# Toeplitz blocks of 64 rows: a channel pair in the row halves of the array, its tables on two DMA queues

## The chip, the core and the metric

The kernel runs on one core of one Trainium2 chip. The metric is device time in microseconds (us) of one launch: the median of three runs before the change is 2316.38 us (2315.62 to 2317.1). A profile is one execution recorded by the hardware profiler; it names PE (TensorE matmul), PEld (TensorE weight load), DVE (VectorE), ACT (ScalarE), POOL (GpSimd) and SP (SyncE, which here only issues DMAs and reads registers).

## What is computed

`x` is 32 sequences of 64 channels of 1024 samples. Four residual layers follow one another; the change lies in the first alone.

```python
def _L0_cond_ref(u, log_dt, C, log_A_real, A_imag, D, length):
    K = _get_kernel(log_dt, C, log_A_real, A_imag, Lq)     # one filter of 1024 taps a channel
    y = jnp.fft.irfft(rfft(u, n=2*Lq) * rfft(K, n=2*Lq)[None], n=2*Lq)[..., :Lq]
    y = y + u * D[:, None]
    mask = (jnp.arange(Lq)[None, :] < length[:, None])
    return y * mask[:, None, :]
...
x = x + _L0_cond_ref(x, ...)                      # causal convolution, masked
x = x + einsum('bsi,boi->bso', x, weight1[ids1])  # an adapter matrix 1024x1024 for each sequence
x = x + einsum('bij,bkj->bik', x, weight2[ids2])  # another
x = x + gated_mlp_with_low_rank_adapters(x)       # the rest of the time
```

## The kernel before

**Stages.** The work falls into the convolution of all 64 channels for all 32 sequences; the two adapter layers of the first chunk of 8 sequences (`adapters(0)`, L297 to L345); and the gated MLP of the four chunks, into which the adapters of later chunks are woven. The profile shows them at 20 to 194 us, 194 to 330 us, and 330 us to the end.

**Making the filters.** `kernels(g)` (L1315) makes the filters of one group of channels; `GROUPS` are 4, 4, 8, 8, 8, 8, 8, 8, 8, here called sets 0 to 8. A set is a loop through several engines: POOL raises powers, DVE reduces an angle (`br`, L1177 to L1181), ACT takes absolute value, sine and cosine with table loads between (`bk` L1186, `bsi` L1328, `bco` L1187 and L1330, `brho` L1249), DVE multiplies (`bet`, `bgt` L1341), PE contracts (`pk`, L1346 and L1355), ACT copies out of PSUM (`ks`, L1364) and issues the store to DRAM (`kp`, L1366). Set g+2 is made while set g is convolved (`more`, L1445).

**Convolving.** A causal convolution is a product with a Toeplitz matrix. `convolve` (L1372) treats 4 channels (`HA`). For each channel it reads from DRAM a table `hk` with one shifted copy of the filter in each partition: partition p starts one sample after partition p-1, so that any 128 columns of it are a 128x128 Toeplitz block. With the reversed samples `uf` as moving operand, 8 matmuls (L1404) of 256, 224, ... 32 columns sum over the block diagonals d = 0 to 7 of one channel. In the profile each such fp32 matmul is two records, so a channel is 16 records on PE, and a pair of channels 32. There are 32 pairs, here numbered 0 to 31. DVE multiplies a pair's PSUM bank by the mask (`tmp`, L1172), POOL adds it to `x` (L1419) for the first chunk, copies the other chunks' share (L1422) and stores it (L1423).

**Order.** PE follows the source order (`manual_schedule(engines={PE})`, L129). The other engines' orders come from a planner. Each engine works through its own list in order, DMA issues among it: an issue that waits holds back everything behind it on that engine. SP issues all of `uf` (a buffer of two), `hk` (a buffer of three pairs) and the adapter weights; ACT issues only the stores `kp`. Eight completion semaphores are taken in turn by the DMAs of SP and ACT together, and a DMA waits for the one eight before it.

**Weights ahead.** Adapter weights are 128 tiles of 512 KB for the first chunk. 9 rotating buffers (`ROTATING`) and a number of resident ones (`early`: `EARLY` of their own and 4 in the place of a later `x` tile; `LATE` more once the filters are made) are filled during the convolution: 36 tiles in all, by `fetch` (L207), whose calls are spread over the convolution by `FIRST_LOADS` and `MORE_LOADS` (L1394 to L1398); what is left is issued after the last table. The other 92 tiles come while `adapters(0)` runs, each when PE has used up a rotating buffer.

Of the kernel before, what the change touches and what calls it, by code (L numbers as in the profile page):

```python
# [9 lines left out]
F32 = mybir.dt.float32  # L10
# [4 lines left out]
SP = mybir.EngineType.SP  # L15
# [4 lines left out]
P = 128  # L20
B, H, L = 32, 64, 1024
NS = 64
KT = L // P
# [8 lines left out]
MB = 4  # L32
MG = 2
NG = FM // MG
EARLY = 16
LEFT_AT = 11
LATE = 7
FIRST_LOADS = 8
MORE_LOADS = 3
ROTATING = 9  # L40
HA = 4
SEG = 2
# [10 lines left out]
KROW = P + L  # L53
# [23 lines left out]
def kernel(  # L77
# [55 lines left out]
    epool = first.enter_context(tc.tile_pool(name="epool", bufs=1, side="right"))  # L133
    early = [epool.tile([P, L], F32, tag=f"e{i}", name=f"early{i}") for i in range(EARLY)]
    early += [
# [75 lines left out]
    def places():  # L211

        lpool = first.enter_context(tc.tile_pool(name="lpool", bufs=1, side="right"))
        for i in range(LATE):
            early.append(lpool.tile([P, L], F32, tag=f"l{i}", name=f"late{i}"))

    convolution(tc, cst, consts, xt, xf, ssm, lens, xs[0], cd, ps_tile, fetch, places)
    for _ in before:
        pass
# [911 lines left out]
def convolution(tc, cst, consts, xt, xf, ssm, lens, x0, cd, ps_tile, fetch, places):  # L1131
# [9 lines left out]

    nc = tc.nc
    with ExitStack() as ctx:
        g0 = ctx.enter_context(tc.tile_pool(name="g0", bufs=1))
        g0_2 = ctx.enter_context(tc.tile_pool(name="g0_2", bufs=2))
        making = ExitStack()
# [2 lines left out]
        s3 = ctx.enter_context(tc.tile_pool(name="s3", bufs=3))  # L1149
# [14 lines left out]
        def small():  # L1164
            n_small[0] += 1
            return s1.tile([P, H], F32, tag=f"sm{n_small[0]}", name=f"sm{n_small[0]}")
# [4 lines left out]
        def tt(o, a, b, op):  # L1171
            nc.vector.tensor_tensor(o, a, b, op)  # L1172
            return o
# [80 lines left out]
        x, y = small(), small()  # L1254
# [6 lines left out]
        t, em, ep = small(), small(), small()  # L1261
# [110 lines left out]
        def convolve(kp, row, ha, between):  # L1372


            uf = s3.tile([P, HA, KT, B], F32, tag="uf", name=f"uf{ha}", bufs=2)
            nc.sync.dma_start(uf, xf[:, ha : ha + HA])
            if ha == 0:
                fetch(FIRST_LOADS)
            tmp = g0_2.tile([P, HA, KT * B], F32, tag="tmp", name=f"tmp{ha}")
            for i in range(0, HA, 2):  # L1380
                hk = s3.tile([P, 2, L], F32, tag="hk", name=f"hk{ha + i}")

                for j in range(0, 2, 1 if ha == 0 else 2):
                    n = 1 if ha == 0 else 2
                    nc.sync.dma_start(
                        hk[:, j : j + n],
                        bass.AP(
                            tensor=kps.tensor,
                            offset=kp[row + i + j : row + i + j + 1, 1:2].offset,
                            ap=[[1, P], [KROW, n], [1, L]],  # L1390
                        ),
                    )

                first, last = ha <= HA * MORE_LOADS, ha > H - HA * MORE_LOADS  # L1394
                if ha and i == 0:
                    fetch(1 + first)
                elif ha and last:
                    fetch(1)  # L1398
                if i:
                    between()  # L1400
                ps = ps_tile(f"pc{ha + i}").rearrange("p (i t) -> p i t", i=2)
                for j in range(2):
                    for d in range(KT):
                        nc.tensor.matmul(  # L1404
                            ps[:, j, d * B :],
                            hk[:, j, d * P : (d + 1) * P],
                            uf[:, i + j, : KT - d, :].rearrange("p k b -> p (k b)"),
                            start=(d == 0),
                            stop=(d == KT - 1),
                        )  # L1410
                tt(
                    tmp[:, i : i + 2, :],
                    ps,
                    maskf.unsqueeze(1).to_broadcast([P, 2, KT * B]),
                    ALU.mult,
                )
            xv = x0.rearrange("p k (b h) -> p k b h", h=H)[:, :, :, ha : ha + HA]
            tv = tmp.rearrange("p i (k b) -> p k b i", b=B)[:, :, :BC, :]
            nc.gpsimd.tensor_tensor(xv, xv, tv, ALU.add)  # L1419
            co = g0.tile([P, NCK - 1, HA * KT, BC], F32, tag="co", name=f"co{ha}")  # L1420
            tv = tmp.rearrange("p i (k c b) -> p c (i k) b", k=KT, b=BC)[:, 1:]
            nc.gpsimd.tensor_copy(co, tv)  # L1422
            nc.gpsimd.dma_start(  # L1423
                cd.rearrange("c p g e -> p c g e")[:, :, ha // HA],
                co.rearrange("p c i b -> p c (i b)"),
            )
# [14 lines left out]
        maskf = mask.rearrange("p k b -> p (k b)")  # L1441
        for g, n in enumerate(GROUPS):
            h0 = sum(GROUPS[:g])

            def more():  # L1445
                if len(ready) < min(g + 3, len(GROUPS)):
                    ready.append(kernels(len(ready)))
                    if len(ready) == len(GROUPS):
                        making.close()
                        places()  # L1450

            for i in range(0, n, HA):
                convolve(ready[g], i, h0 + i, more)
# [20 lines left out]
def _layouts(np, v):  # L1474
    cont = np.ascontiguousarray

    x = v["x"]

    xt = x.reshape(NCK, TC, KT, P).transpose(3, 0, 2, 1)

    xf = x.reshape(B, H, KT, P)[..., ::-1].transpose(3, 1, 2, 0)

    def states(a):
        return np.concatenate([a.T, a.T])
# [58 lines left out]
    for i, (m0, m1) in enumerate(BLOCKS):  # L1543
        n = 2 * (m1 - m0)
        ad[:, i, :, :n] = a[:, :, :, m0:m1].reshape(NE, P, n, R)
    left = left.reshape(P + REST, NE, R).transpose(1, 0, 2)
    n = 2 * BLOCKS[0][1]
# [71 lines left out]
```

## Time and profile before

The profiled execution has a span of 2313.8 us, 2.6 us under the median of the runs.

| what | from | value |
|---|---|---|
| PE, PEld busy over the span | the page's part 1 | 2249.8 us (97%), 1868.0 us (81%) |
| DVE, ACT, POOL busy | part 1 | 1320.6, 380.0, 270.6 us |
| mean granted TensorE clock | cores | 0.998 |
| all DMA | part 3 | 684.96 MB, 296 GB/s |
| `hk` tables | part 6, DMA view | 30 of 1024 KB, 8.8 us to landing; 4 of 512 KB, 6.6 us |
| `kp` stores on ACT's queue | DMA view | 7 of 32 KB, 7.9 us to landing; 2 of 16 KB, 3.2 us |
| `uf`, `early` loads | DMA view | 512 KB each, 5.8 and 9.4 us to landing |
| DVE mask product `tmp` | groups | 32 of 688 ns |
| first and last convolution matmul | tile view of `pc` | start at 29.1 and 193.8 us |

In the rows of groups the columns are line, engine, operation, output and inputs by name, shape, count; then busy time in us and the mean of one in ns; then idle time of the engine just before, with what ended it. In a timeline a row is start, duration, engine, line, operation, operands, count, and in brackets the idle time before it with its cause.

### The profile page before, as it was taken

To read this page: it belongs to the slowest core of one execution; us is meant where nothing else is said; L and a number is where in the kernel's file an instruction comes from. 1 tells how busy PE (TensorE), PEld (TensorE's weight loads), DVE (VectorE), ACT (ScalarE), POOL (GpSimd) and SP (SyncE) were. 2 spreads that over 40 slices of the span, in tenths; PEclk is the share of its full clock that TensorE was granted. 3 is DMA by queue.
4 is the path that set the end of the run, shared out by engine and by line. 5 is a ranking of instruction groups with operands and counts; after the bars stand their busy time and mean duration, and the time that the engine had idled before them with its cause. 6 is when DMAs were issued, how large, how long until landed. Compare 5 with 4: busy or idle time off the path is not lost.

```text
span 2313.8 us, 53743 instructions
## 1 busy us (share of the span) xinstructions
PE 2249.8 (97%) x21706; PEld 1868.0 (81%) x21706; DVE 1320.6 (57%) x2791; ACT 380.0 (16%) x822; POOL 270.6 (12%) x388
## 2 busy tenths in 40 slices
PE   5999989999999999999999999999999999999999
PEld 4996557787777789688778889688769889799998
DVE  7511127567446776546535676646535676477585
ACT  4300001011001112111102212121102212121220
POOL 3423003111101121000000011000000011100000
PEclk9999999999999999999999999999999999999999
DMA  8999997879997957879997957879997947285582
GB/s 306 354 370 394 407 403 280 317 289 354 365 343 293 350 174 258 304 285 360 350 357 279 358 167 265 297 292 358 355 351 288 363 152 276 87 298 203 191 280 68
DMA packets 201802, 684.96 MB, mean 296 GB/s; under 512 B 26178, under 2 KB 28482, under 8 KB 201042
## 3 DMA queue, kind: packets, MB, share of 16 engines
q1 hardware_dynamic: 169714, 590.77, 69.5%
q0 software_dynamic: 25184, 82.37, 9.6%
q10 hardware_dynamic: 6656, 8.39, 1.0%
q8 instruction: 171, 2.80, 0.5%
q14 instruction: 77, 0.63, 0.1%
HBM read 614.02 MB, written 67.40 MB: 295 GB/s over the span
## 4 chain that ended last, share of the span: by engine, by line
PE 78%; DMA 14%; issue 5%; DVE 2%; POOL 1%; POOLq 0%; SPq 0%; ACT 0%; DVEq 0%
PE pq L664 28%; PE po L1063 22%; PE pa L304 11%; DMA wa<-in_w 7%; PE pc L1404 5%; PE pf L573 5%; PE pr L797 3%; DMA wa<-sums 2%; DMA sums<-kept 1%; PE pe L456 1%; DMA hk<-kp 1%; PE pl_d L427 1%; DMA kp<-ks 1%; DMA wf<-in_wg 0%; DMA wr<-in_wr 0%
## 5 line engine op out<-in xcount | busy, mean ns | idle before, releaser
L304 PE MATMUL pa<-wa,x 128*32 128x256 f32 x7760 | 449.1, 381 | 19.3 <-DMA wa<-in_w 16.8
L664 PE MATMUL pq<-xd,wa 128*128 128x128 f32 x3360 | 415.9, 275 | 1.3 <-DMA wa<-sums 0.9
L304 PEld LDWEIGHTS pa<-wa,x 128*32 128x32 f32 x7760 | 241.8, 110 | 209.9 <-DMA wa<-in_w 49.1
L664 PEld LDWEIGHTS pq<-xd,wa 128*128 128x128 f32 x3360 | 395.0, 192 | 2.3 <-DMA wa<-sums 2.2
L664 PE MATMUL pq<-xd,wb 128*128 128x128 f32 x2520 | 324.1, 276 | 0.6 <-DVE x L316 0.4
L664 PEld LDWEIGHTS pq<-xd,wb 128*128 128x128 f32 x2520 | 300.7, 192 | 4.7 <-DVE x L316 0.6
L314 DVE STREAM_TRANSPOSE y<-pa 128x512 f32<-128x512 f32 x64 | 45.9, 717 | 286.6 <-PE pa L304 286.6
L1063 PE MATMUL po<-act,wd 128*128 128x256 f32 x640 | 168.6, 386 | 0.0
L1404 PE MATMUL pc<-uf,hk 128*128 128x256 f32 (+7 forms) x1024 | 153.3, 312 | 12.2 <-DMA hk<-kp 9.5
L1063 PE MATMUL po<-actd,s 128*128 128x256 f32 x640 | 164.2, 379 | 0.0
L1063 PE MATMUL po<-actd,wd 128*128 128x256 f32 x640 | 164.2, 379 | 0.0
L1404 PEld LDWEIGHTS pc<-uf,hk 128*128 128x128 f32 x1024 | 148.4, 195 | 16.6 <-issue 7.9
L355 POOL DMA_INDIRECT bgu<-in_bgu,rows x44 | 51.4, 1168 | 924.0 <-PE pe L456 827.2
L573 PE MATMUL pf<-xd,wf 128*128 128x256 f32 x640 | 150.9, 381 | 0.0
L1063 PEld LDWEIGHTS po<-act,wd 128*128 128x128 f32 x640 | 117.8, 190 | 29.9 <-issue 14.6
L482 DVE TENSOR_TENSOR s<-wd 128x256 f32<-128x256 f32 x80 | 33.8, 423 | 184.1 <-PE po L1063 184.0
L573 PEld LDWEIGHTS pf<-xd,wf 128*128 128x128 f32 x640 | 121.2, 191 | 17.4
L1063 PEld LDWEIGHTS po<-actd,s 128*128 128x128 f32 x640 | 121.6, 190 | 16.5
L1063 PEld LDWEIGHTS po<-actd,wd 128*128 128x128 f32 x640 | 121.6, 190 | 16.5
L1095 ACT COPY uo<-po 128x256 f32<-128x256 f32 x48 | 17.9, 373 | 622.3 <-PE po L1063 620.2
L573 PE MATMUL pf<-xd,s 128*128 128x256 f32 x480 | 115.9, 385 | 3.9 <-DVE up L607 2.7
L573 PEld LDWEIGHTS pf<-xd,s 128*128 128x128 f32 x480 | 91.0, 191 | 20.0 <-DVE up L607 4.4
(235 smaller groups left out, 2566.4 us busy)
## 6 DMA issues: line engine op xcount, KB each, us to landing
wa<-in_w SPq DMA_DIRECT2D x485, 512.0 KB, 7.0
wa<-sums SPq DMA_DIRECT2D x210, 512.0 KB, 5.8
wb<-parts SPq DMA_DIRECT2D x120, 384.0 KB, 5.3
wd<-in_wd SPq DMA_DIRECT2D x80, 512.0 KB, 7.0
wb<-in_wq SPq DMA_DIRECT2D x90, 384.0 KB, 5.9
hk<-kp SPq DMA_DIRECT2D x30, 1024.0 KB, 8.8
sums<-kept POOLq DMA_DIRECT2D x30, 1024.0 KB, 7.2
wf<-in_wg SPq DMA_DIRECT2D x20, 512.0 KB, 7.1
```

Of the source, the lines that this page charges most:

```text
L304: nc.tensor.matmul(acc[i * S : (i + 1) * S, s * 256 : (s + 1) * 256], xs[c][:, kt, lo + s * S : lo + (s + 1) * S], wt[:, i * 256 : (i + 1) ...
L314: nc.vector.transpose(y, acc)
L355: nc.gpsimd.indirect_dma_start(out=t, out_offset=None, in_=table, in_offset=bass.IndirectOffsetOnAxis(ap=at_, axis=0),)
L427: nc.tensor.matmul(ps[pair(j)], at[:, i, pair(j)], x_i[:, 2 * H * j : 2 * H * (j + 1)], start=(i == 0), stop=(i == n - 1),)
L456: nc.tensor.matmul(ps[:, at_ * 2 * H : (at_ + 1) * 2 * H], bt[pair(j), g], tms[table][pair(j)], start=(g == 0), stop=True, skip_group_chec ...
L482: nc.vector.tensor_add(s1, a21, a22)
L573: nc.tensor.matmul(ps, ws[j][:, kt, :], xb[j][:, kt, :], start=start and kt == 0, stop=kt == KH - 1, skip_group_check=True,)
L664: nc.tensor.matmul(ps[:, to * TQ : (to + 1) * TQ], w[i][:, k, :], xb[:, j, SLOT[i], k, :], start=start and k == 0 and to == 0, stop=k == K ...
L797: nc.tensor.matmul(ps, wts[i][:, kt, :], xs[c][:, kt, :], start=(kt == 0), stop=(kt == KT - 1),)
L1063: nc.tensor.matmul(pss[j], *term, start=(s0 == m0 and i == 0 and home[j] % 2 == 0), stop=(end and i == len(terms) - 1 and not late), skip_ ...
L1095: nc.scalar.copy(u1, p1)
L1404: nc.tensor.matmul(ps[:, j, d * B :], hk[:, j, d * P : (d + 1) * P], uf[:, i + j, : KT - d, :].rearrange("p k b -> p (k b)"), start=(d == ...
```

## The change

A channel's table gets 64 partitions of 1088 samples (64 + 1024) in place of 128 of 1024, and two channels share one tile: the even channel in partitions 0 to 63, the odd one in 64 to 127. The even channel's half is issued by SP and the odd one's by ACT. The blocks are now 64 rows high: each channel takes 16 matmuls of 64 rows, in place of 8 of 128, with the widths 256, 256, 224, 224, ... 32, 32; those of the two channels alternate, each pair into two PSUM banks (one for each half) that serve two pairs. The two mask products of 4 channels follow both pairs. `xf` is laid out anew on the host to fit. Tables get 4 buffers. `EARLY` rises by 2, so that 38 weight tiles are loaded ahead, and `fetch` is called once for each pair but the first two. SP's order in this stage becomes that of the source.

```diff
-EARLY = 16
+EARLY = 18
...
-MORE_LOADS = 3
+PAIR = 2
+HP = P // PAIR
...
     with ExitStack() as ctx:
+        ctx.enter_context(tc.manual_schedule(engines={SP}))
...
-            uf = s3.tile([P, HA, KT, B], F32, tag="uf", name=f"uf{ha}", bufs=2)
-            nc.sync.dma_start(uf, xf[:, ha : ha + HA])
+            uf = s3.tile([P, HA // PAIR, 2, KT * B], F32, tag="uf", name=f"uf{ha}", bufs=2)
+            nc.sync.dma_start(uf, xf[:, ha // PAIR : (ha + HA) // PAIR])
             if ha == 0:
                 fetch(FIRST_LOADS)
...
-            for i in range(0, HA, 2):
-                hk = s3.tile([P, 2, L], F32, tag="hk", name=f"hk{ha + i}")
-
-                for j in range(0, 2, 1 if ha == 0 else 2):
-                    n = 1 if ha == 0 else 2
-                    nc.sync.dma_start(
-                        hk[:, j : j + n],
+            halves = [slice(r * HP, (r + 1) * HP) for r in range(PAIR)]
+            banks = [ps_tile(f"pc{ha}_{r}").rearrange("p (i t) -> p i t", i=HA // PAIR) for r in range(PAIR)]
+            for i in range(HA // PAIR):
+                hk = s3.tile([P, HP + L], F32, tag="hk", name=f"hk{ha}_{i}", bufs=4)
+                for r in range(PAIR):
+                    h = row + PAIR * i + r
+                    (nc.sync, nc.scalar)[r].dma_start(
+                        hk[halves[r]],
                         bass.AP(
                             tensor=kps.tensor,
-                            offset=kp[row + i + j : row + i + j + 1, 1:2].offset,
-                            ap=[[1, P], [KROW, n], [1, L]],
+                            offset=kp[h : h + 1, 1:2].offset,
+                            ap=[[1, HP], [1, HP + L]],
                         ),
                     )
-
-                first, last = ha <= HA * MORE_LOADS, ha > H - HA * MORE_LOADS
-                if ha and i == 0:
-                    fetch(1 + first)
-                elif ha and last:
+                if ha:
                     fetch(1)
                 if i:
                     between()
-                ps = ps_tile(f"pc{ha + i}").rearrange("p (i t) -> p i t", i=2)
-                for j in range(2):
-                    for d in range(KT):
+                for e in range(-1, PAIR * KT - 1):
+                    k0 = (e + 1) // 2
+                    for r in range(PAIR):
                         nc.tensor.matmul(
-                            ps[:, j, d * B :],
-                            hk[:, j, d * P : (d + 1) * P],
-                            uf[:, i + j, : KT - d, :].rearrange("p k b -> p (k b)"),
-                            start=(d == 0),
-                            stop=(d == KT - 1),
+                            banks[r][:, i, k0 * B :],
+                            hk[halves[r], (e + 1) * HP : (e + 1) * HP + P],
+                            uf[halves[r], i, e % 2, : (KT - k0) * B],
+                            start=(e < 0),
+                            stop=(e == PAIR * KT - 2),
+                            skip_group_check=True,
                         )
+            for r in range(PAIR):
                 tt(
-                    tmp[:, i : i + 2, :],
-                    ps,
-                    maskf.unsqueeze(1).to_broadcast([P, 2, KT * B]),
+                    tmp.rearrange("p (i r) t -> p r i t", r=PAIR)[:, r],
+                    banks[r],
+                    maskf.unsqueeze(1).to_broadcast([P, HA // PAIR, KT * B]),
                     ALU.mult,
                 )
...
-    xf = x.reshape(B, H, KT, P)[..., ::-1].transpose(3, 1, 2, 0)
+    xf = x.reshape(B, H // PAIR, PAIR, KT, 2, HP)[..., ::-1]
+    xf = xf.transpose(2, 5, 1, 4, 3, 0).reshape(P, H // PAIR, 2, KT * B)
```

## The prediction, made before the changed kernel had run

> **What bounds the kernel now.** I first cut the time into stretches by the stages (start:end, length, busy us of each engine with counts, clock, DMA share, GB/s).
>
> ```profile
> 20.00:82.00 62.00, 49.27 (x371) 47.53 (x371) 45.28 (x81) 32.04 (x50) 31.22 (x38) 0.97 0.88 320
> 82.00:194.00 112.00, 108.86 (x792) 105.95 (x791) 23.54 (x37) 6.15 (x11) 29.76 (x36) 1.00 0.99 375
> 194.00:330.00 136.00, 124.16 (x2067) 68.30 (x2067) 22.77 (x38) 4.08 (x4) 16.79 (x29) 1.00 1.02 401
> ```
>
> Three bounds follow one another. From 82 to 194 us PE is busy 109 of 112 us, with the DMA full beside it. From 194 to 330 the DMA is the bound: it moves 401 GB/s, while PE, though it looks busy, waits for tile after tile. Before 82 us neither is full; there the filter sets, made on DVE and ACT (45 and 32 of 62 us), set when a table can be read. After 330 us both programs list the same instructions in the same order, so a shift there passes to the end. Next PE's timeline, then the chain of waits:
>
> ```profile
> 57.46 9.36 PE L1404 MATMUL pc<-uf,hk 128*128 128x256 f32 x64 [0.62 <-DMA hk<-kp]
> 70.36 11.01 PE L1404 MATMUL pc<-uf,hk 128*128 128x256 f32 x64 [3.55 <-DMA hk<-kp]
> 81.30 0.69 PE L1346 MATMUL pk<-bet,bgt 128*32 128x32 f32 x16
> ...
> 81.97 18.59 PE L1404 MATMUL pc<-uf,hk 128*128 128x256 f32 x128
> ```
> ```profile
> 318.77 9.95 DMA wa<-in_w
> 328.76 1.07 PE pa L304 x16
> ```
>
> 128 records are four pairs, so a pair costs 18.51/4 = 4.63 us. Pair 9 starts at 81.97. From there three blocks of four pairs with a filter contraction take 19.19 us each, and eleven pairs 50.9: 108.5 us. The convolution ended at 194.1, so only 194.1 - 82.0 - 108.5 = 3.6 us were lost to waits after pair 9. The second fence shows the adapters' end: the last tile is issued at 318.77, lands 9.95 us later, and PE finishes 1.07 us after.
>
> **The change, part by part.**
>
> *Bytes.* A pair's table falls from 2 x 128 x 4096 B = 1.05 MB to 2 x 64 x 4352 B = 0.56 MB: 15.7 MB over 32 pairs, 39 us at 401 GB/s. That would be the gain if all of it were on the path. It isn't: from 82 to 194 us PE decides, and what is loaded ahead is limited by buffers, 38 tiles for 36.
>
> *Matmuls.* A pair now takes 64 records for 32, with the same widths, each on half the rows. Side by side they cost 4.63 us as before, one after another about twice that. The nearest rows are the low-rank expansion, four 32-row groups alternating, 128 columns, and the full-array matmul of 128 columns before it:
>
> ```profile
> 335.38 2.05 PE L331 MATMUL pr<-x,wr 128*128 128x128 f32 x16
> 337.36 1.39 PE L456 MATMUL pe<-tm_g,bgu 32*128 32x128 f32 x32
> ```
>
> Full-array: 2.05/16 = 128 ns a record. Row groups: 1.39/32 = 43 ns, so at least three run at once. I take the two halves as side by side, 4.63 us a pair: no gain and no loss. The bounds are 4.63 and 64 x 0.128 = 8.2 us.
>
> [...]
>
> *Second queue.* [...] Thirty-two issues at 0.31 us (the `kp` row) are added to the engine that makes the filter sets, and each waits in order behind the activations ahead of it:
>
> ```profile
> 59.60 0.63 ACT L1186 ACTIVATE bk<-br 128x512 f32<-128x512 f32 x1 [3.82 <-DVE br L1181]
> 60.25 1.28 ACT L1328 ACT_TABLE_LOAD   x1
> 61.55 0.42 ACT L1328 ACTIVATE bsi<-br 128x256 f32<-128x256 f32 x1
> 61.87 0.71 ACT L1187 ACTIVATE bco<-bk,cst 128x512 f32<-128x512 f32 x1
> ```
>
> `bk` of sets 4 to 8 starts at 50.16, 59.60, 68.94, 78.11 and 87.09: a period of 9.2 us through DVE, half of the 18.5 us in which PE uses a set up; so this order matters until set 8 is done, and then no more. In the new order pair 5's ACT half stands behind `brho` that follows set 4, pair 6's behind `bsi` of set 5, pair 7's behind `bco` of set 6, pair 8's behind `bk` of set 7, pair 9's behind `bk` of set 8; then come pairs 10 to 12 at once. I take the sets 1 us earlier than before, since mask products leave their way. The third set's absolute value now precedes `kp` of set 2, which slips from 37.1 to 42.5 us; with 5 to 7 us to landing (4.94 and 7.53 in the trace) pair 4's halves go out near 49 and come near 53, just when PE gets there.
>
> A half is 278 KB. To landing: below, 4 us (first `hk` of 512 KB at an idle queue, 25.14 to 29.1); above, 8 us (`kp` on ACT's queue beside a full SP queue). I take 4, since SP's queue is shorter now. Issue, landing and PE's work, us:
>
> | pair | ACT issues | lands | PE free | PE starts |
> |---|---|---|---|---|
> | 5 | 54.8 | 58.8 | 58 | 58.8 |
> | 6 | 61.0 | 65.0 | 63.4 | 65.0 |
> | 7 | 70.9 | 74.9 | 69.6 | 74.9 |
> | 8 | 77.7 | 81.7 | 81.3 | 81.7 |
> | 9 | 86.7 | 90.7 | 87.0 | 90.7 |
>
> (Pair 7 gets 1.8 us more, as the pairs after the old 3.55 us wait took 11.01 for 9.26 us; 0.7 for the contraction behind 4 and 8.) Pair 9 starts at 90.7 for 81.97: 8.7 us late. From pair 10 on ACT issues a half as soon as the table four pairs back is used, 13.9 us ahead, and no wait is left: the 3.6 us go. The end of the convolution: 90.7 + 108.5 = 199.2, 5.1 us later. Traffic of 0.56 + 0.26 + 0.52 + 0.2 MB a pair (tables, `uf`, a tile, `cd`) in 4.63 us is 333 GB/s, below the 375 measured, so PE stays the bound there. SP's waits in source order (`uf` on PE two groups back, tables behind it, 9.3 us ahead) stay covered. The index load `il` with its conversions is moved up into SP's and DVE's early lists, ahead of set 3's products: landing 9.5 us after 32 us, near 41 as DVE reaches it at 39; 0 to 2 us, I take 0, ending in the range.
>
> *Tail.* Two mask products behind the last pair for one: +0.7 us. `adapters(0)` starts at 195.76 + 5.8 = 201.5.
>
> *Adapters.* It took 195.76 to 329.83, 134.1 us. Two tiles fewer: 2 x 1.28 = 2.6 us (0.524 MB at the 409 GB/s of the DMA view for the second half of this stretch). The seven late tiles, the last of which landed at 200.3, are no longer outstanding: 4.5 us. Against that the first refill's latency is no longer covered, about 1 us. So 128 us, and the end is at 329.5 for 329.83. PE alone would need 16 x 7.04 + 5.5 = 118, so 128 has cover; the DMA stays the bound.
>
> Sum: +5.1 + 0.7 - 6.1 = -0.3 us on the span of 2313.8, which lies 2.6 us under the median: 2316, no change. The unknowns give 3 to 8 us for a landing (-1 to +4), 1 us for the sets either way, 123 to 131 us for the adapters: 2308 to 2324.
>
> **Rivals.**
>
> *The tables no longer wait* (24%). If ACT's place in the list costs nothing, because the halves come before PE asks, PE runs through from pair 1 at 36.6 us: 31 x 4.63 + 7 x 0.65 = 148.1, end at 184.7, adapters from 187.0, end 315: 15 us less, 2301. For it: halved tables, four buffers. Against it: the ACT rows above.
>
> *The row halves disturb each other* (20%). The place is L1404's successor; the price is what a pair takes beyond 4.63 us, times the 23 pairs from pair 9 on. At 0.2 us a pair (4%) it adds 4.6 us and decides for slower; fully one after another it is 23 x 3.6 = 83 us, 2399. For it: 64 loads for 32 a pair, in 64-row groups that no row of the trace shows. Against it: the 43 ns of L456. Most of its chance lies at small prices, 2320 to 2335.
>
> *A late half each time* (4%): 8 us to landing and SP held by ACT's semaphores, 2324.
>
> **Numbers.** My case has 52%: 9 faster, 33 same, 10 slower. The second adds 23 to faster and 1 to same; the third 19 to slower and 1 to same; the last 3 and 1. A measurement here tells 0.2% (4.6 us) from no change. Faster 0.32, same 0.36, slower 0.32. The range, 2301 to 2332, takes in the first rival and the small prices of the second; my case's own is 2308 to 2324.
>
> **What would show it.** Pair 9 starting near 91 us with PE's wait before pairs 7 and 9 ended by `hk`, after ACT's `bk` rows: right. Pairs of 4.6 us after that: right about the halves; more: the second rival. The convolution's end near 199, the adapters in 128 us. I am wrong if PE never waits after 40 us, or if the adapters take under 123 us.

## The result, and the profile after

The changed kernel takes 2332.65 us (median of four runs, 2329.27 to 2338.86) where the kernel before, on the same chip, took 2316.59 (2315.62 to 2317.1). The ratio is 1.0083, with a 95% interval of 1.0061 to 1.0105: **slower by 0.8%**, just above the range of 2301 to 2332. The profiled execution is the one of 2329.27 us; its span is 2327.6 us, 13.8 more than before.

First the stretches of the changed kernel (start:end, length, busy us of PE, PEld, DVE, ACT and POOL with counts, granted clock, DMA share, GB/s):

```profile
20.00:82.00 62.00, 46.87 (x578) 44.18 (x578) 40.34 (x83) 34.57 (x52) 27.66 (x35) 0.94 0.80 222
82.00:194.00 112.00, 102.26 (x1344) 100.66 (x1344) 19.78 (x36) 6.35 (x11) 26.75 (x33) 0.95 1.01 273
194.00:330.00 136.00, 127.62 (x2091) 83.17 (x2089) 23.46 (x34) 4.08 (x4) 21.70 (x35) 0.99 0.94 355
```

The middle row holds the surprise. The DMA engines are as full as before (1.01, then 0.99), yet they move 273 GB/s where they moved 375. A share says how long packets were under way, not how much they carried; read the two columns together. PE's timeline of the changed kernel shows who waits for it (start, length, engine, line, tiles, records, and in brackets the idle time ahead and who ended it; a pair has 64 records now):

```profile
71.00 11.13 PE L1403 MATMUL pc<-uf,hk 64*128 64x256 f32 x128 [4.25 <-DMA hk<-kp]
...
90.72 20.33 PE L1403 MATMUL pc<-uf,hk 64*128 64x256 f32 x254 [2.12 <-DMA hk<-kp]
...
118.39 15.76 PE L1403 MATMUL pc<-uf,hk 64*128 64x256 f32 x192 [1.96 <-DMA hk<-kp]
...
140.42 9.48 PE L1403 MATMUL pc<-uf,hk 64*128 64x256 f32 x128 [0.88 <-DMA hk<-kp]
...
161.53 9.48 PE L1403 MATMUL pc<-uf,hk 64*128 64x256 f32 x128 [1.05 <-DMA hk<-kp]
...
185.16 9.48 PE L1403 MATMUL pc<-uf,hk 64*128 64x256 f32 x128 [1.76 <-DMA hk<-kp]
```

Pair 9 starts at 90.72, as predicted. But from there PE goes on waiting for tables, every second or third pair, to the end of the convolution at 216.4 us (194.1 before). The page's row for these matmuls sums it up (busy us, mean ns | idle before, by whom):

```profile
L1403 PE MATMUL pc<-uf,hk 64*128 64x256 f32 (+7 forms) x2048 | 165.1, 319 | 20.1 <-DMA hk<-kp 20.1
```

In the kernel before it read 153.3 us busy and 12.2 idle, 9.5 of it for `hk`. So PE waits more, and is also busy 12 us longer. The second part goes with a lower granted clock: 0.94 and 0.95 in the first two stretches, for 0.97 and 1.00 before. From 90.72 us to the end of the convolution the clock records have four spans of 3.4 us at half the clock, each beginning 0.2 to 1.1 us after one of these waits; not every wait has one. Where nothing waits, the new matmuls take 4.62 us a pair (a_gather, below), as the old ones did.

The adapters then run from 218.7 to 349.0 us, 130.4 us for the forecast 128, and end 19.2 us later than before. Of these, 13.8 are left at the end of the span. In the experiments below the shift also changes over the unchanged rest, by -10 to +3 us and mostly downwards, so a part of such a delay is taken back later; where, was not followed.

### The profile page after: what moved, and what is told of

Read it like the earlier page. It is cut to its first block, busy times and chain, and to the rows that moved or that the text cites. A ratio compares the mean times of both kernels' runs of the same rounds, so it can differ in the third digit from the quotient of the medians.

```text
span 2327.6 us, 55844 instructions
## 1 busy us (share of the span) xinstructions
PE 2258.6 (97%) x22730; PEld 1880.5 (81%) x22730; DVE 1313.5 (56%) x2791; ACT 382.8 (16%) x824; POOL 269.5 (12%) x388
## 4 chain that ended last, share of the span: by engine, by line
PE 78%; DMA 7%; issue 3%; DVE 1%; POOL 1%; POOLq 0%; SPq 0%; DVEq 0%
PE pq L665 28%; PE po L1064 23%; PE pa L305 13%; PE pf L574 6%; DMA wa<-in_w 6%; PE pr L798 3%; PE pe L457 2%; DMA sums<-kept 1%; PE pl_d L428 1%; DMA wr<-in_wr 0%; DMA wb<-parts 0%; PE pl_g L428 0%; PE pl_u L428 0%; PE po L1072 0%; POOL sums L549 0%
## 5 line engine op out<-in xcount | busy, mean ns | idle before, releaser
L1403 PE MATMUL pc<-uf,hk 64*128 64x256 f32 (+7 forms) x2048 | 165.1, 319 | 20.1 <-DMA hk<-kp 20.1
L1403 PEld LDWEIGHTS pc<-uf,hk 64*128 64x128 f32 x2048 | 160.5, 197 | 24.1 <-issue 9.2
L574 PEld LDWEIGHTS pf<-xd,s 128*128 128x128 f32 x480 | 90.7, 190 | 19.6 <-DVE up L608 4.5
```

The source lines that it names most:

```text
L574: nc.tensor.matmul(ps, ws[j][:, kt, :], xb[j][:, kt, :], start=start and kt == 0, stop=kt == KH - 1, skip_group_check=True,)
L1403: nc.tensor.matmul(banks[r][:, i, k0 * B :], hk[halves[r], (e + 1) * HP : (e + 1) * HP + P], uf[halves[r], i, e % 2, : (KT - k0) * B], sta ...
```

## The experiments

All ratios are to runs of the kernel before on the same chip, with 95% intervals. "Half" is a transfer into partitions 0 to 63 or 64 to 127, "whole" one into all 128. The ends of the convolution and of the adapters are from the trace (before: 194.1 and 329.8 us).

| run | tables, queue, weight tiles fetched | ratio | conv. ends | adapters end |
|---|---|---|---|---|
| after | half, SP and ACT, one a pair | 1.0083 [1.0061, 1.0105] | 216.4 | 349.0 |
| a_sp | half, SP, one a pair | 1.0074 [1.0052, 1.0096] | 216.9 | 350.7 |
| a_few | half, SP and ACT, one in two pairs | 1.0077 [1.0049, 1.0105] | 206.7 | 349.4 |
| a_sp_few | half, SP, as before | 1.0026 [1.0014, 1.0038] | 198.2 | 336.5 |
| a_full_sp | whole, one half unread, SP, one a pair | 1.0057 [1.0038, 1.0076] | 209.9 | 346.5 |
| a_full_few | whole, one half unread, SP, as before | 1.0024 [1.0013, 1.0035] | 196.8 | 334.9 |
| b_split | before, each table in two halves | 1.0287 [1.0270, 1.0304] | 266.8 | 402.7 |
| b_even | before, in even and odd partitions | 1.0055 [1.0035, 1.0076] | 203.3 | 339.6 |
| b_wide | before, rows of 4352 bytes | 1.0006 [0.9996, 1.0016] | 194.3 | 331.3 |
| b_two | before, second channel on ACT | 1.0058 [1.0041, 1.0074] | 208.1 | 343.6 |
| b_src | before, SP in source order, one tile a pair | 1.0036 [1.0017, 1.0054] | 205.8 | 340.6 |
| b_fetch | before, one tile a pair | 1.0037 [1.0025, 1.0050] | 207.0 | 341.7 |

### What makes full engines slow

The first of four kernels undoes the second queue:

```diff
-                    (nc.sync, nc.scalar)[r].dma_start(
+                    nc.sync.dma_start(
```

> The changed kernel with both halves of a table on SP's queue. My theory now: from 82 to 194 us the DMA engines are full in the changed kernel and yet move only 273 GB/s (375 before), and this, not ACT's list, holds PE. What makes them slow is open: (T1) a transfer into 64 of the 128 partitions, (T2) two queues that take turns on the same engines, (T3) rows of 4352 bytes where there were 4096. T2: back to 360-380 GB/s, convolution ends near 195 us instead of 215, time 2308-2316 us. T1 or T3: still 265-290 GB/s; pair 9 starts near 83-86 us instead of 90.7, since no half waits behind ACT's activations, but the convolution still ends at 208-215 us; time 2324-2333 us. Rival (T4), that ACT's order alone costs the time and the full engines are a by-product: convolution ends near 203 us, time 2318-2322, with more than 330 GB/s.

The other three put one suspect each into the kernel before: halves, wide rows, two queues.

```diff
 b_split
-                        hk[:, j : j + n],
+                        hk[r * 64 : r * 64 + 64, j : j + n],      # r = 0, 1, both on SP
 b_wide
-                            ap=[[1, P], [KROW, n], [1, L]],
+                            ap=[[1, P], [KROW, n], [1, L + 64]],  # rows of DRAM 64 longer
 b_two
-                    nc.sync.dma_start(                            # one channel each
+                    (nc.sync, nc.scalar)[j].dma_start(
```

> The kernel before, each table transfer of 128 partitions cut into two of 64 partitions, both on SP, one after the other; same bytes, same rows of 4096 bytes, same matmuls. T1 (64 partitions): 270-300 GB/s from 82 to 194 us, and the 42 MB of that stretch take 28-40 us more: time 2335-2355 us. T2 or T3: within 0.3% of the kernel before, 370-380 GB/s.

> The kernel before with rows of 1088 samples (4352 bytes) loaded where 1024 are used, all 128 partitions, one queue. T3 (long rows): a row takes about 280 ns of an engine instead of 170, 256 rows a pair over 16 engines is 1.8 us a pair more, 30-40 us over the stretch: time 2340-2355 us. T1 or T2: only the 6% more bytes of the tables, 2.1 MB in all, 0-5 us: time 2316-2322 us.

> The kernel before with whole tables of 128 partitions, the first channel of a pair on SP and the second on ACT. T2 (two queues): 270-300 GB/s from 82 to 194 us, convolution ends 25-40 us later: time 2335-2355 us. T1 or T3: GB/s of that stretch near 370; ACT's order makes pairs 5 to 9 late, pair 9 at 88-92 us instead of 82, convolution ends at 198-202 us, of which the adapters' stretch takes some back: time 2316-2322 us.

a_sp took 2334.38 us, b_split 2383.76, b_wide 2315.01, b_two 2331.21. The stretch from 82 to 194 us of each, first a_sp:

```profile
82.00:194.00 112.00, 102.31 (x1256) 96.72 (x1253) 19.73 (x33) 4.69 (x9) 27.74 (x34) 0.94 1.03 274
```

b_split:

```profile
82.00:194.00 112.00, 84.54 (x566) 80.96 (x566) 13.08 (x23) 4.17 (x8) 20.86 (x27) 0.91 1.01 255
```

b_wide:

```profile
82.00:194.00 112.00, 108.23 (x789) 105.41 (x788) 22.02 (x36) 5.78 (x11) 29.38 (x36) 1.00 1.00 385
```

b_two:

```profile
82.00:194.00 112.00, 101.86 (x734) 98.54 (x733) 28.26 (x52) 11.97 (x18) 29.90 (x37) 0.97 0.97 364
```

The last two columns decide. Wide rows and two queues leave the rate at 385 and 364 GB/s; one queue does not bring it back (274). Halves alone, with the old bytes, rows and matmuls, bring it down to 255 at full engines. b_two's loss of 0.58% does not come from the rate; where it comes from is not settled. Its pair 9 starts at 85.5 us, 3.5 late, while the convolution ends 14 us late, and two of its waits for `hk`, 3.78 and 2.67 us, come only at 165 and 190 us, where I had expected none. b_split cost more than I expected, 68 us for 28 to 40, since I had slowed only one stretch; its convolution ends 73 us later.

The same can be seen finer. The transfers' view of a window lists GB/s in 40 slices. The kernel before, 97 to 190 us:

```profile
GB/s 418 386 296 418 406 383 264 411 416 407 326 419 409 337 247 418 418 419 298 420 408 321 252 405 423 377 386 400 411 351 241 340 421 421 411 409 414 407 403 414
```

and b_split in the same window:

```profile
GB/s 238 337 285 231 275 222 229 352 255 226 278 229 229 351 304 274 237 231 271 233 347 303 226 227 241 356 247 250 226 226 259 365 226 222 226 226 224 379 217 224
```

Two plateaus: about 418 with whole tables and 226 with halves. b_split's slices rise to between 337 and 379 in seven places, where, as I take it, weights or inputs pass (13 loads of 512 KB in that window). What a half misses could be the partitions or the number of rows. So b_even cuts each table in two of 64 rows as well, but by even and odd partitions:

```diff
-                        hk[:, j : j + n],
+                        hk[r : P : 2, j : j + n],                 # r = 0, 1, both on SP
```

Were the partitions the cost, I expected 2313 to 2325 us, about as before, and 360 GB/s or more from 82 to 194 us.

> The kernel before, each table transfer cut in two of 64 rows as in b_split, but one takes the even partitions and the other the odd ones, so that each reaches over the whole 128. [...] Rival R (64 rows in a transfer are the cost, wherever they lie): like b_split, 2375-2390 us and about 255 GB/s.

```profile
82.00:194.00 112.00, 106.88 (x777) 103.80 (x777) 18.03 (x30) 4.17 (x8) 28.06 (x36) 0.98 0.97 363
```

363 GB/s, and packets of 4096 bytes at a median of 159 ns as before: 64 rows run at nearly the rate of whole tables (375) if they are spread over all partitions. So which partitions a transfer reaches is what counts here, and not its number of rows. By the two plateaus a half runs at 226 of 418 GB/s, 54%; why, no run shows. Nor do transfers into the two halves add up to a whole one: a_sp and the changed kernel, which fill both halves of a pair from one queue or from two, move 274 and 273 GB/s with other transfers between.

b_even, at 2325.17 us, is still 0.55% slower than before. Its one long wait, 9.73 us ahead of pair 8 (3.55 before, ahead of pair 7), lies where the engines are not full (share 0.77 from 20 to 82 us), so it is not the rate; I did not follow it further.

The packets' own times in these traces, from 97 to 190 us (a_gather, told below, from 130 to 190):

```
SP's queue, median ns of a packet        4096 bytes     4352 bytes (tables)
before                                      159              -
b_even                                      159              -
b_split                                     280              -
after (tables on ACT's queue: 246)          248             285
a_sp_few                                    241             294
a_full_few                                  159             168
a_gather (tables on POOL's queue)           159             168
```

In b_split most packets of 4096 bytes are tables. In the changed kernel none is: 4096 bytes are weights and inputs, which go to all 128 partitions, and they too take 248 ns for 159. The halves slow the loads that pass beside them; with whole tables and the same order of fetches (a_full_few) these are back at 159. The stores `cd` on POOL's queue, which go the other way, to DRAM, hardly change: 165 ns for 159. From 97 to 215 us the tables' 2,496 packets took 41 us of engine time, of which 12 would be saved at a_full_few's mean of 183 ns, and SP's 3,871 others took 59 us, of which 18 would be saved at their 172 ns there.

### Twice the bytes, and the fetch rhythm

a_full_sp fills every channel's table over all 128 partitions, though PE reads only one half of it: 1.11 MB a pair for 0.56. a_few fetches fewer weight tiles. b_src puts SP's new order and rhythm into the kernel before.

```diff
 a_full_sp
-                        hk[halves[r]],
+                        hk[:, r],                                 # both on SP, 3 buffers, EARLY = 16
-                            ap=[[1, HP], [1, HP + L]],
+                            ap=[[1, P], [1, HP + L]],             # r = 1 starts 64 samples earlier
 a_few
-                if ha:
+                if ha and i == 0:
                     fetch(1)
 b_src
+        ctx.enter_context(tc.manual_schedule(engines={SP}))
-                if ha and i == 0:
-                    fetch(1 + first)
-                elif ha and last:
-                    fetch(1)
+                if ha:
+                    fetch(1)
```

Were the partitions the cost, a_full_sp was to be back at the kernel before in spite of twice the bytes: 2312 to 2322 us, 370 GB/s or more, the convolution's end at 194 to 203 us. The estimate: at some 400 GB/s 1.11 MB take 2.8 us, where 0.56 MB at b_split's 226 took 2.5.

> The changed kernel's matmuls in row halves, but each channel's table filled over all 128 partitions, of which PE reads one half: 1.11 MB a pair instead of 0.56, both on SP, three table buffers for four and 16 early tiles for 18. [...] Rival B (bytes count, or the row halves of the array are what is slow): no faster than the changed kernel, 2330-2350 us.

> The changed kernel with one weight tile fetched for two pairs in the convolution instead of one for each (the rest are asked for behind it). If the sum of the DMA engines' time sets the end of the adapters (tables at half rate: as much engine time for half the bytes, plus the slowing of what is beside them), the convolution ends earlier, at 200-208 us instead of 215, but the adapters' end stays at 344-352 us (349 in the changed kernel, 330 before) and the time at 2326-2338 us. Rival: the waits of PE in the convolution are the loss, and the DMA has room: the adapters end at 332-340 us, time 2316-2324 us.

> The kernel before with the order of the changed one on SP alone: SP in source order, one weight tile fetched for every pair. Theory: of the loss of 16 us none comes from this part: 2312-2320 us, convolution ends at 192-198 us. Rival: the order on SP holds the tables back, as in the changed kernel: convolution ends at 205 us or later, time 2325 us or more.

a_full_sp took 2326.76 us, a_few 2332.26, b_src 2323.21. The stretch from 82 to 194 us of a_full_sp:

```profile
82.00:194.00 112.00, 103.20 (x1340) 99.00 (x1340) 19.88 (x33) 4.69 (x9) 28.94 (x36) 0.97 1.00 391
```

The rate is back at 391 GB/s, and twice the bytes are not slower than half of them (a_sp: 1.0074, intervals overlapping). But the kernel before is not reached, and b_src says why: **the rhythm alone costs 0.36%**. I had expected nothing of it. Its stretch:

```profile
82.00:194.00 112.00, 100.36 (x710) 97.08 (x708) 19.68 (x33) 5.25 (x10) 24.12 (x31) 0.97 0.98 376
```

Whole tables, full engines at the old rate, and PE busy 100 us for 109: with a weight tile for every pair there is more to move than fits beside PE, 1.05 + 0.26 + 0.2 + 0.52 = 2.03 MB in 4.63 us, 438 GB/s, where the engines moved 401 at their best stretch. The halves, which cost the engines as much as whole tables (306 us of work up to the adapters' end in a_sp_few, 310 in a_full_few, in the table below), are in the same place. b_fetch parts the rhythm from the fixed order:

> The kernel before with one weight tile fetched for every pair, SP's order left to the scheduler as it was (b_src without its fixed order). If b_src's loss of 0.4% is the fetch rhythm (1.05 + 0.26 + 0.2 + 0.52 MB a pair in 4.63 us would be 438 GB/s, more than the 401 that the adapters' stretch moves): 2318-2326 us. If it is the fixed order on SP: 2311-2318 us.

2323.51 us, 0.37%: it is the rhythm. a_few shows that the old rhythm alone does not mend the change: its convolution ends 10 us earlier, but its adapters, with fewer tiles loaded ahead, at the same time, 349.4 us.

Two runs that did not tell: the changed kernel and its twin with whole tables, both on SP, with the old rhythm and SP's order left to the scheduler.

```diff
-        ctx.enter_context(tc.manual_schedule(engines={SP}))
-                if ha:
-                    fetch(1)
+                if ha and i == 0:
+                    fetch(1 + first)
+                elif ha and last:
+                    fetch(1)
```

> The changed kernel with both halves on SP and, for the weight tiles, the fetch rhythm and SP's order of the kernel before; so only the halved tables and the row halves are left of the change. Theory (a half table takes the DMA engines about as long as a whole one, so nothing is saved, and it slows what is beside it): 2316-2330 us, convolution ends at 195-206 us, adapters at 335-347 us. Rival (the fetch for every pair is the whole loss, the halves do no harm): 2305-2315 us, adapters end before 330 us, since 15.7 MB fewer are moved.

> The same, but each table filled over all 128 partitions (1.11 MB a pair, half of it unread); of the change only the matmuls in row halves are left. Theory (the row halves of TensorE are innocent): 2310-2320 us, within 0.3% of the kernel before, and not slower than a_rh in spite of twice the bytes. Rival (row halves cost on PE): 2325 us or more.

2339.63 and 2337.25 us (1.0113 [1.0084, 1.0143] and 1.0107 [1.0086, 1.0128]). Both missed, and not by the halves, since the twin with whole tables lost as much. DMA's share falls to 0.87 and 0.95 from 82 to 194 us, and there are new waits. From a_rh's timeline of PE:

```profile
104.16 12.32 PE L1406 MATMUL pc<-uf,hk 64*128 64x256 f32 x128 [5.90 <-DMA uf<-in_xf]
124.26 6.23 PE L1406 MATMUL pc<-uf,hk 64*128 64x256 f32 x64 [7.78 <-issue]
```

The inputs `uf` come late, with the engines not full. So they were run again with SP's source order kept (without the first line of that diff):

> The changed kernel with both halves on SP, SP in source order, and the fetch rhythm of the kernel before (one or two weight tiles for two pairs). Theory (a half table costs the DMA engines as much as a whole one and slows what is beside it): slower than the kernel before by 0.5-1%, 2326-2338 us, adapters end at 343-352 us. Rival (the doubled fetch rhythm is the loss): within 0.3% of before, 2308-2320 us.

> The same with each channel's table filled over all 128 partitions, 1.11 MB a pair, half of it unread: of the change, the row halves on TensorE and SP's source order are left. Theory (whole-range transfers run at full rate, row halves are innocent): 2312-2322 us, faster than a_sp_few with twice the bytes, 82 to 194 us at 360 GB/s or more. Rival (row halves or the order cost): as slow as a_sp_few.

2319.8 and 2318.75 us: 0.26% and 0.24% slower, their intervals nearly the same. The forecast for halves, 0.5 to 1%, fell; the rival's size held. In a_sp_few the engines are still full at 273 GB/s, but fewer weights are asked for, and PE gets its tables:

```profile
82.00:194.00 112.00, 109.06 (x1475) 106.03 (x1474) 21.20 (x35) 4.69 (x9) 29.65 (x37) 0.98 1.02 273
```

PE's 109.06 us are the 108.86 of the kernel before. Undoing the second queue alone (a_sp) or the rhythm alone (a_few) brings nothing, undoing both brings two thirds. So beside halves that cost what whole tables cost, either of the two is enough for most of the loss: the rhythm, which counts on their being cheaper, or ACT's list. In a_few it is ACT's list that remains: the run differs from a_sp_few in the queue, and little in the rhythm, the main part of pair 9 starts at 92.7 us for 82.1, and the engines' share from 20 to 82 us is 0.65 for 0.77.

Where the lateness at the adapters' end lies shows a sum over all packets from 20 us to that end: how long the 16 engines worked (mean of one, us), and the rest, idle. (Packets overlap a little: from 97 to 190 us b_split's queues add up to 103.5% of the 16 engines, so a full engine counts up to 1.04.)

| run | worked | idle | idle from 15 us before the convolution's end to 8 after |
|---|---|---|---|
| before | 305 | 5 | 0 |
| after | 311 | 18 | 11 |
| a_few | 308 | 21 | 0 |
| a_sp_few | 306 | 11 | 0 |
| a_full_few | 310 | 5 | 0 |
| b_split | 383 | 0 | 1 |
| b_fetch | 299 | 22 | 15 |

The 16 MB that the halves save the changed kernel spare no engine time; it works 6 us more and stands idle 13 us more, which are the 19. Most of that idle time lies where a tile for every pair has used up the buffers too soon. SP issues the last of the tiles that fit at 200.03 us, and the next at 219.35, when the adapters free buffers; between, PE works off the pairs that came late. From 195 to 219 us, the kernel before, the changed one and b_fetch:

```profile
195.00:219.00 24.00, 23.24 (x432) 14.05 (x436) 5.07 (x12) 1.04 (x1) 12.45 (x22) 1.00 1.02 382
195.00:219.00 24.00, 21.28 (x272) 20.70 (x276) 3.47 (x6) 0.00 (x0) 6.09 (x8) 0.93 0.63 185
195.00:219.00 24.00, 22.88 (x264) 17.75 (x268) 3.73 (x10) 0.00 (x0) 7.21 (x12) 0.88 0.40 143
```

So the rhythm costs twice: full engines (0.98 from 82 to 194 us in b_fetch) make tables late, and then, with all tiles in, the engines have little to do (0.40 from 195 to 219 us) while PE catches up.

### The saved bytes, at full rate

One gather on POOL's queue, by a list of 128 row starts, fills both halves of a pair in one transfer over all partitions:

```diff
-                for r in range(PAIR):
-                    h = row + PAIR * i + r
-                    (nc.sync, nc.scalar)[r].dma_start(
...
+                h = row // PAIR + i
+                nc.gpsimd.indirect_dma_start(
+                    out=hk,
+                    out_offset=None,
+                    in_=bass.AP(tensor=kp.tensor, offset=0, ap=[[1, kp.shape[0] * KROW], [1, 1]]),
+                    in_offset=bass.IndirectOffsetOnAxis(ap=at[:, h : h + 1], axis=0),
+                )
```

Each filter set has a DRAM tile of its own for it. a_gather keeps a fetch for every pair, a_gather_few has the old rhythm.

> The changed kernel with one transfer for both halves of a pair: a gather on POOL's queue by a list of 128 row starts, so that 0.56 MB go to all 128 partitions at once. Theory (the halves' range is the cost): the tables then cost half the engine time, so DMA's share falls below 1 or its rate returns to 360 GB/s or more between 100 and 194 us; convolution ends at 195-205 us, adapters at 320-335 us, time 2302-2318 us. [...]

> The gather with the fetch rhythm of the kernel before. [...]

I expected a_gather_few within 6 us of a_gather, its convolution ending 0 to 5 us earlier; for both, were the gather itself slow, 2325 us or more and the convolution's end after 210 us. It ended at 204.8 us in a_gather and at 205.7 in a_gather_few.

2318.25 us (1.0023 [1.0013, 1.0033]) and 2318.97 (1.0016 [1.0006, 1.0027]). In the sum over all packets up to the adapters' end the 16 engines worked 305 us for 116 MB in the kernel before, 306 for 100 MB in a_sp_few, and 274 for 100 MB in a_gather. **The same bytes cost 31 us less when they are not aimed at one half.** Once the tables come in time, PE does not wait; a_gather's timeline of PE:

```profile
80.46 11.88 PE L1407 MATMUL pc<-uf,hk 64*128 64x256 f32 x128 [5.74 <-DMA hk<-kp,at]
...
153.96 50.79 PE L1407 MATMUL pc<-uf,hk 64*128 64x256 f32 x704
```

704 records are 11 pairs in 50.79 us, 4.62 us a pair, as the full-array matmuls took (50.9). The loss lies ahead of it: pairs wait for POOL's list, which also makes the filter sets' exponents. So two kernels use halves on SP for the first pairs and the gather from pair 8 or from pair 12 on:

```diff
+                if ha < sum(GROUPS[:NEAR]):     # NEAR = 3 in a_mix3, 4 in a_mix4
...
+                else:
+                    nc.gpsimd.indirect_dma_start(
...
```

> Halves on SP with the old fetch rhythm for the first eight pairs, while POOL still makes the filter sets' exponents; from pair 8 on one gather over all 128 partitions for both halves of a pair, and a weight tile fetched for every pair. In a_gather the steady pairs ran at 4.62 us without a wait (eleven in 50.79 us) and the engine time up to the adapters' end fell from 305 to 274 us; what it lost lay before pair 12. Theory: the convolution ends at 193-200 us, adapters at 324-333 us, time 2306-2316 us. Rival (POOL's list delays the first gathers): convolution ends at 203 us or later, as slow as a_gather, 2316-2322 us.

> The same with the gather from pair 12 on, when POOL has made all exponents. Theory: convolution ends at 193-198 us, adapters at 324-332 us, 2306-2315 us, so no slower than the kernel before. Rival: the later stretch is bound by the adapters' own bytes and the 38 tiles that fit, so nothing of the saved engine time reaches the end: 2314-2320 us.

2317.61 us (1.0019 [1.0009, 1.0029]) and 2321.81 (1.0042 [1.0028, 1.0056]): no better. From a_mix3's timeline of PE:

```profile
84.03 6.55 PE L1417 MATMUL pc<-uf,hk 64*128 64x256 f32 x64 [11.28 <-issue]
```

The first gather comes 11 us late (9.4 in a_mix4). PE's row names no releaser, but POOL's list shows the gather of pair 8 behind the sum, copy and store of pairs 6 and 7, and that sum waiting for their mask product:

```profile
75.27 1.21 POOL L1434 TENSOR_TENSOR x<-x,tmp 128x256 f32<-128x256 f32 x1 [5.33 <-DVE tmp L1175]
...
78.01 0.96 POOL L1438 DMA_DIRECT2D cd<-co  x1 [0.30 <-POOL co L1437]
79.28 1.05 POOL L1404 DMA_INDIRECT hk<-kp,at  x1 [0.30 <-DMA early<-in_w]
```

An earlier place in POOL's list was not tried. And the adapters last 132.5 us in a_mix3, 135.7 before, though the engines were busy only 0.90 of the time while PE worked. No version beat the kernel before.

## Why the prediction was wrong, step by step

The time lies only just above the range, but the mechanism was wrong: the upper part of the range was there for row halves that disturb each other, which did not happen.

- **What failed**: "Traffic of 0.56 + 0.26 + 0.52 + 0.2 MB a pair (tables, `uf`, a tile, `cd`) in 4.63 us is 333 GB/s, below the 375 measured, so PE stays the bound there". It counted a half's bytes at the rate of whole transfers. A half's packet takes 246 to 294 ns where a whole one's takes 168, and the packets beside it 248 where they took 159. The stretch moved 273 GB/s, less than the 333 needed, so the DMA bounds it. From pair 9 to the end PE took 216.4 - 90.7 = 125.7 us for the forecast 108.5: 17 us, nearly all of the 19 by which the adapters end late. Of the 17, 8.7 are waits for `hk`; most of the rest is the lower clock (0.95 granted over these 125.7 us, an estimate of some 7 us), which the forecast left out after pair 9.
- **The price of a half** had no row to be read from: none in the prediction is of a transfer into 64 partitions. At b_split's 226 GB/s for 418, as an estimate, 0.56 MB in halves cost what 1.04 MB cost whole, and the sum would have been near b_src's: 2.02 MB in 4.63 us, 435 GB/s, above the 401 that the trace moved.
- **ACT's list** did hold tables back, and pair 9 was forecast at 90.7 and went on at 90.72. That the number fits so well is in part luck: pair 5 started at 61.46 for 58.8, and the long wait came ahead of pair 6 (71.00 for 65.0) and not of pair 7. It did not decide by itself. In a_sp pair 9 starts at 79.9 us, 11 earlier, and the convolution ends at 216.9 all the same, since its engines are full from 82 to 194 us (share 1.03) and move 274 GB/s there.
- **Row halves side by side** was right: 4.62 us a pair where nothing waits (forecast 4.63), and no gain from hidden weight loads: in the kernel before L1404's loads were busy 148.4 us and its matmuls 153.3 us within 165 us, so they ran beside each other already. The rival in which they disturb each other falls with it.
- **Bytes not on the path** fits what was seen, but no run tests it cleanly: a_gather saves 31 us of engine time and gains nothing, its engines idle for 43 us where they were for 5, but a part of that lies at POOL's list.
- **The adapters** took 130.4 us for 128, from a start 17 us later than forecast. Loading all tiles ahead was counted as a gain of 4.5 us; that the engines would then stand idle until the adapters begin was not counted.
- **The rivals**: that tables no longer wait came out the other way; that a late half costs a wait each time describes the timeline, but its cause was the rate and not the lateness.

Open are the 0.25% of a_sp_few and a_full_few, whose convolution ends 3 to 4 us later than before and whose adapters end 5 to 7 later: a_sp_few's engines are idle 5 us more, and those of a_full_few, with 2 MB more to move, work 6 us more, but neither was tested by a change. Open, too, is what takes back a part of the shift after the adapters, and where b_two's loss arises.

## What to carry to other kernels

Price a transfer by its packets, and ask which partitions it reaches: halving the bytes by filling only 64 partitions at a time saved no engine time here (311 us up to the adapters' end for 305 before). Where a profile's DMA share is 1 and its GB/s falls, look at the transfers' shape before the queues. And a faster fetch rhythm that spends a saving is itself a change: test it alone, since here it cost 0.37% in the old kernel, and ask what the engines do once the buffers are full.

## What was unexpected in the hardware

The transfers into one half of the partitions also slowed the whole-range loads beside them: their packets of 4096 bytes went from a median of 159 ns to 241 (a_sp_few) and 248 (the changed kernel). Filling the whole range of which half goes unread (1.11 MB a pair) took hardly more engine time up to the adapters' end, 310 us (a_full_few), than the two halves alone (0.56 MB), 306 us (a_sp_few).
